# Two half exchanges through DRAM joined into one pair, in a gated graph network

## The chip, the cores and the metric

One core of a Trainium2 chip. The metric is the device time of one execution in microseconds. The kernel before took 1796.03 us in the median of three runs (1793.29 to 1797.85).

## What is computed

Sixteen graphs ("batches") of 1024 nodes with 128 features each, and a symmetric 0/1 adjacency matrix per graph. First a layer norm with relu and four layers of a gated graph network (GRU); then layer norm, relu, and four graph convolutions with batch norm over all graphs. Both results are added to the running `x`. The change lies in the GRU part:

```python
def _gru_cell(m, h, w_ih, w_hh, b_ih, b_hh):
    ...
    r = jax.nn.sigmoid(xr + hr)
    z = jax.nn.sigmoid(xz + hz)
    n = jnp.tanh(xn + r * hn)
    return (1.0 - z) * n + z * h
...
h = x
for i in range(L):                                     # L = 4
    hw = jnp.einsum('bnc,cd->bnd', h, weight[i])
    m = jnp.einsum('bjn,bjd->bnd', adj, hw)
    h = _gru_cell(m, h, w_ih[i], w_hh[i], b_ih[i], b_hh[i])
```

## The kernel before, in words

The path that runs is `exact_path`; a second, general path stands behind a flag and isn't entered. The kernel keeps `h` transposed (128 features on partitions, 1024 nodes along the row), in two halves of 512 nodes. The weight is folded into the input gates (`w_mT`), so that a layer first aggregates `h` over the adjacency and then runs the gates.

**Two streams.** `sa` takes the even batches and `sb` the odd ones. One `half_step(one, two)` runs the gates of stream `two` for its layer (`gate_step` for each half, L972 on TensorE: 24 matmuls) and then the aggregation of stream `one` for its next layer (`agg_step`, L525: 32 matmuls). Half steps alternate the roles. A batch takes four layers, so eight half steps make a round in which both streams change their batch, and there are seven such changes (fourteen batch ends, all but the last two batches).

**What the aggregation needs.** Its weights are `ghw`: `h` with the nodes on partitions, split into a high part (rounded, cast on ScalarE, L905) and a low part (the difference, on VectorE, L906). TensorE takes for each block of 128 nodes two matmuls of the high part and two of the low part, so it needs the low part of the first half two matmuls after the high one.

**The turn through DRAM.** For layers 1 to 3 the turn from features to nodes is made in two moves: VectorE transposes 32x32 blocks (`t_h`, L711), and SP dumps the result into a DRAM buffer (`exchange_out`, L591: one issue of 256 KB per half) and fetches it back with the blocks in another order (`exchange_in`, L598: four issues of 64 KB per half, each for 32 partitions). The buffers are called `cross_h`, the fetched tiles `n_h`. `half_away` makes the dumps after each half of the gates, `halves_back` issues the eight fetches at the start of the stream's next half step, and `split_back` makes `ghw` from them.

**The change of batches.** When a stream has done its fourth layer, `finish` does the same exchange for two more things: the coming batch's normalized `x` (`take`: `y_in` to `t_in` to `cross_in` to `h_in`), which the next gates read as `h`; and the last `h` of the batch that ends (`t_out` to `cross_out` and back into its own tile `h`), which VectorE adds to `x` in the tail (`tail_sums`, L732). `blocks_out` makes the two dumps of each. The fetches are put on an agenda with `at(clock[0] + 1, ...)`: those of `h_in` come first in the next half step (`due("ins")`), those of `h` after the first half of its gates and after the first dump of `half_away` (`due("outs")`).

**What sets the order.** In the steady part, the orders of TensorE, GpSimd and SP are those in which the program is written (`manual_schedule(engines=PE, Pool, SP)`). ScalarE's and VectorE's are chosen by a scheduler from its own cost estimates, so a change in the DMA issues can move instructions on these two. All SP issues stand in one queue: besides the exchanges, the row loads of the coming batch into `stage` (L573, eight per batch of 512 KB each, four buffers, so that the second four wait for the casts of the first), and DMA transposes of adjacency rows (L610). GpSimd casts each loaded row (L578, `row<-stage`) and each row to be transposed (L609, `half<-row`). ScalarE's `glance` (L587, `junk<-stage`) and VectorE's `look` (L604) test the loaded rows.

**DMA semaphores.** The issues of SP take eight completion semaphores in turn, so an issue also waits until the eighth issue before it has landed.

Of the kernel before, what the change touches and what calls it, by code (L numbers as in the profile page):

```python
# [8 lines left out]
F32 = mybir.dt.float32  # L9
# [7 lines left out]
P = 128  # L17
HALF = 512
# [323 lines left out]
def exact_path(  # L342
# [21 lines left out]
    nc = tc.nc  # L364
# [3 lines left out]
    NH = N // HALF  # L368
# [26 lines left out]
    def half_tile(name):  # L395
        return keep.tile([P, N], BF16, tag="half", name=name, bufs=8)
# [67 lines left out]
    turned = {}  # L464
# [69 lines left out]
    with ExitStack() as st:  # L534
        work = st.enter_context(tc.tile_pool(name="work", bufs=2))
        rawd = st.enter_context(tc.tile_pool(name="rawd", bufs=2, space=bass.MemoryType.DRAM))
# [49 lines left out]
                k = b * NB + j  # L586
                nc.scalar.activation(junk, lows, AF.Copy, accum_out=low[:, k : k + 1])  # L587

        def exchange_out(t, name):
            d = rawd.tile([P, HALF], F32, tag="cross", name=f"cross_{name}", bufs=8)  # L590
            nc.sync.dma_start(d, t)  # L591
            return d

        def exchange_in(d, t):

            src = d.rearrange("(t r) (s x) -> s r t x", t=4, s=4)
            for s in range(4):
                nc.sync.dma_start(t[s * 32 : (s + 1) * 32, :].rearrange("r (t x) -> r t x", t=4), src[s])  # L598

        def look(b, row, j, part=0):  # L600

            lows = row.bitcast(U16).rearrange("p (n t) -> p n t", t=2)[:, :, 0]
            k = (b + part * B) * NB + j
            nc.vector.tensor_reduce(low[:, k : k + 1], lows, axis=AX.X, op=ALU.max)  # L604
# [95 lines left out]
        def by_nodes(cols):  # L700
            return cols.rearrange("c (q k i) -> c k q i", q=4, i=32)

        def four_ways(cols):
            return cols.rearrange("p (k a c) -> p k a c", a=4, c=32)

        def blocks_out(src, name):

            return [half_out(cross_tile(f"t_{name}_{hf}"), src, hf, name)[0] for hf in range(NH)]

        def half_out(t, src, hf, name):  # L710
            turned = nc.vector.transpose(by_nodes(t), four_ways(src[:, hf * HALF : (hf + 1) * HALF]))  # L711
            return exchange_out(t, f"{name}_{hf}"), turned

        def cross_tile(name):
            return half_tile(name).bitcast(F32)
# [32 lines left out]
        def last_tail(b, xt, hT):  # L748
            nt = tail_sums(b, xt, hT)
            y = y_mid(b) if b + 1 < B else xt.rearrange("p k c -> p (k c)")  # L750
            store_xmid(b, xt)

            def rest():
                norm_apply(xt, y, nt)
                store_ymid(b, y)

            return rest
# [10 lines left out]
        class Stream:  # L768
# [105 lines left out]
            def take(self):  # L874
                self.xt, self.y = self.next_x, self.next_y
                self.across = True
                self.hT = work.tile([P, N], F32, tag="h", name=f"h_in{self.b}", bufs=7)
                return blocks_out(self.y, f"in{self.b}")
# [5 lines left out]
            def half_away(self, hf):  # L884

                if self.turned_away(self.i + 1 - hf):
                    nm = f"{self.b}_{self.i + 1 - hf}"
                    out, self.last_dve = half_out(cross_tile(f"t_h{nm}_{hf}"), self.new, hf, f"h{nm}")
                    self.outs.append(out)

            def halves_back(self):
                nm = f"{self.b}_{self.i}"
                self.backs = [cross_tile(f"n_h{nm}_{hf}") for hf in range(NH)]
                for d, t in zip(self.outs, self.backs):
                    exchange_in(d, t)
                self.hw = hw_tiles(self.b, f"ghw{nm}")
# [107 lines left out]
            def finish(self):  # L1004

                if self.i < L:
                    return
                args = self.b, self.xt, self.hT
                self.b, self.i = self.b + 2, 0
                if self.b >= B:  # L1010
                    self.rest = last_tail(*args)
                    return
                ins = self.take()
                h_in = self.hT
                outs = blocks_out(args[-1], f"out{args[0]}")
                parts = [args[-1][:, hf * HALF : (hf + 1) * HALF] for hf in range(NH)]

                def arrive(ds, ts):
                    for d, t in zip(ds, ts):
                        exchange_in(d, t)  # L1020

                at(clock[0] + 1, "ins", lambda: arrive(ins, [h_in[:, :HALF], h_in[:, HALF:]]))
                at(clock[0] + 1, "outs", lambda: arrive(outs, parts))
                self.plan(clock[0], (*args, parts))

        clock = [3]

        def at(n, place, go):
            agenda.setdefault((n, place), []).append(go)
# [268 lines left out]
    def first_weights(b, pm, stats):  # L1298

        mt = work.tile([P, N], F32, tag="h", name=f"cm{b}", bufs=3)  # L1300
        pc = [acc(t, f"pw{b}_{t}") for t in ("g_hn", "g_xn")]
        for hf in range(NH):
            cols = slice(hf * HALF, (hf + 1) * HALF)
            nc.scalar.copy(mt[:, cols], pm[hf])
            nc.tensor.matmul(pc[hf], w_c[:, 0, :], mt[:, cols], start=True, stop=True)
        return conv_done(b, 0, pc, stats)
# [70 lines left out]
    for b in range(B):  # L1377
# [4 lines left out]
        if waiting:  # L1382
            last = first_weights(*waiting, stats)
# [52 lines left out]
    for b in range(B):  # L1436
# [3 lines left out]
        for n0, n in pieces(b):  # L1440
# [5 lines left out]
            tag = turns[count % len(turns)]  # L1446
# [10 lines left out]
@with_exitstack  # L1457
def kernel(ctx: ExitStack, tc: tile.TileContext, *args):
    nc = tc.nc
    flagp = ctx.enter_context(tc.tile_pool(name="flagp", bufs=1))  # L1460
    flag_i = flagp.tile([1, 1], I32, tag="flag", name="flag_i")
    exact_path(tc, flag_i, *args)
    inexact = nc.values_load(flag_i, min_val=0, max_val=1 << 24)  # L1463
    with tc.If(inexact > 0):
        general_path(tc, *args)
# [41 lines left out]
```

## Time and profile before

| | before |
|---|---|
| median of 3 runs | 1796.03 us |
| span of the profiled execution | 1795.0 us |
| GRU part (to about 1130 us): TensorE busy | 1109.9 us |
| fetches of `h_in` from `cross_in` | 112 issues, 64 KB each, 2.2 us to landing (median) |
| fetches of `h` from `cross_out` | 112 issues, 64 KB each, 2.0 us |
| dumps `cross_in`, `cross_out` | 28 each, 256 KB, 6.8 and 7.0 us |
| fetches of `n_h` | 360 issues, 64 KB each, 2.0 us |

The profiled execution's own time is known by its span, from the first to the last instruction; the median of the runs lies 1.0 us above it. In the profile, a line such as `L525 PE MATMUL pm<-row,ghw` names the source line, the engine, the operation and the tiles, output first. In a timeline, the first two columns are start and duration in microseconds, `xN` says how many like instructions were merged, and the bracket is how long the engine had been idle and what ended the wait. PE is TensorE, PEld its weight load, ACT ScalarE, DVE VectorE, POOL GpSimd; `SPq` are issues of SP's queue. In a table by stretches, each engine has its busy time and its instructions.

### The profile page before, as it was taken

How to read it: one execution, taken by the hardware profiler on the slowest of the kernel's cores; microseconds unless marked ns; L12 is line 12 of the kernel's file. 1: busy time of each engine (PE TensorE's matmuls, PEld its weight loads, DVE VectorE, ACT ScalarE, POOL GpSimd, SP SyncE). 2: the span in 40 equal slices, each digit the busy share in tenths (PEclk: the TensorE clock that was granted, in tenths of full speed). 3: DMA queues.
4: the chain of work that ended last, by engine and by line, in shares of the span. 5: the costliest groups of instructions: out<-in, count | busy, mean ns of one | idle time of the engine just before them, and what ended most of it. 6: DMA issues, size and time to landing. Idle time of an engine off the chain costs nothing. (4 is left out here: it accounts for less than half of the span.)

```text
span 1795.0 us, 22286 instructions
## 1 busy us (share of the span) xinstructions
PE 1763.4 (98%) x6742; PEld 1194.0 (67%) x6742; DVE 1258.8 (70%) x2308; ACT 1107.2 (62%) x1717; POOL 389.4 (22%) x417
## 2 busy tenths in 40 slices
PE   9999999999999999999999999999999999999997
PEld 6555565556565556556556555677778888888886
DVE  7567867867776776777786776676666666666665
ACT  5346456556556555755655655477777767768765
POOL 4213322332332331422342333110100000000011
PEclk9999999999999999999999999999999999999999
DMA  7448676776676766766767667778866566767667
GB/s 253 112 125 268 171 223 237 200 207 225 205 211 211 236 191 193 263 197 168 263 185 209 241 194 209 268 277 299 284 223 244 209 244 215 246 223 240 241 220 263
DMA packets 363968, 399.11 MB, mean 222 GB/s; under 512 B 159820, under 2 KB 240496, under 8 KB 363840
## 3 DMA queue, kind: packets, MB, share of 16 engines
q1 hardware_dynamic: 343088, 322.54, 57.1%
q0 software_dynamic: 20224, 74.80, 11.5%
q8 instruction: 55, 0.90, 0.2%
q14 instruction: 73, 0.60, 0.1%
q10 hardware_dynamic: 528, 0.26, 0.0%
HBM read 266.95 MB, written 96.99 MB: 203 GB/s over the span
## 5 line engine op out<-in xcount | busy, mean ns | idle before, releaser
L525 PE MATMUL pm<-row,ghw 128*128 128x512 f32 x2048 | 505.6, 403 | 11.8 <-ACT ghw L905 11.1
L525 PEld LDWEIGHTS pm<-row,ghw 128*128 128x128 f32 x2048 | 384.3, 189 | 124.5 <-issue 26.5
L525 PE MATMUL pc_m<-wide,chw 128*128 128x512 f32 x1024 | 246.1, 396 | 0.0
L609 POOL CAST half<-row 128x1024 bf16<-128x1024 f32 x128 | 148.8, 1171 | 327.2 <-DMA adjT<-half 312.5
L525 PEld LDWEIGHTS pc_m<-wide,chw 128*128 128x128 f32 x1024 | 190.5, 188 | 42.3 <-issue 4.3
L991 ACT ACTIVATE z<-g_z,brz 128x512 f32<-128x512 f32 x128 | 87.5, 684 | 171.3 <-PE g_z L972 171.2
L525 PE MATMUL pc_g_r<-wide,chw 128*128 128x512 f32 x464 | 187.0, 403 | 0.3 <-ACT chw L502 0.3
L578 POOL CAST row<-stage 128x1024 fp32r<-128x1024 f32 x112 | 131.5, 1181 | 243.6 <-DMA stage<-in_adj_dram 221.1
L525 PE MATMUL pc_g_z<-wide,chw 128*128 128x512 f32 x464 | 181.0, 390 | 0.0
L985 DVE SCALAR_TENSOR_TENSOR r<-g_hn,vecs,r 128x512 f32<-128x512 f32 x128 | 95.0, 742 | 118.3 <-ACT r L984 76.6
L1237 DVE CAST wide<-block 128x1024 fp32r<-128x1024 bf16 x160 | 109.8, 692 | 73.2 <-PE pc_m L525 46.2
L1237 DVE CAST wide<-packed 128x1024 fp32r<-128x1024 bf16 x160 | 110.2, 691 | 72.1 <-PE pc_g_z L525 53.9
L944 ACT COPY m<-pm 128x512 f32<-128x512 f32 x128 | 68.5, 586 | 147.9 <-PE pm L525 147.9
L990 ACT ACTIVATE r<-r,vecs 128x512 f32<-128x512 f32 x128 | 91.8, 717 | 104.0 <-DVE r L986 104.0
L997 DVE TENSOR_TENSOR h<-h,r 128x512 f32<-128x512 f32 x96 | 81.8, 852 | 101.6 <-ACT r L990 101.6
L1235 ACT CAST wide<-packed 128x1024 fp32r<-128x1024 bf16 x96 | 100.6, 1048 | 59.1 <-PE pc_m L525 28.3
L972 PE MATMUL g_r<-m,w_mT 128*128 128x512 f32 x256 | 131.5, 595 | 2.8 <-ACT m L944 2.3
L1235 ACT CAST wide<-block 128x1024 fp32r<-128x1024 bf16 x96 | 100.6, 1049 | 52.3 <-PE pc_g_z L525 27.7
L972 PE MATMUL g_xn<-m,w_mT 128*128 128x512 f32 x256 | 130.7, 592 | 0.0
L972 PE MATMUL g_z<-m,w_mT 128*128 128x512 f32 x256 | 130.7, 592 | 0.0
L998 DVE TENSOR_TENSOR h<-h,z 128x512 f32<-128x512 f32 x128 | 118.7, 931 | 4.8 <-ACT z L991 1.9
L1285 DVE BATCH_NORM_STATS2 stats<-feat 128x6 f32<-128x512 f32 x128 | 84.1, 686 | 47.0 <-ACT feat L1284 45.9
(187 smaller groups left out, 2804.3 us busy)
## 6 DMA issues: line engine op xcount, KB each, us to landing
block<-adjT_d SPq DMA_DIRECT2D x256, 256.0 KB, 4.7
packed<-adjT_d SPq DMA_DIRECT2D x256, 256.0 KB, 5.5
stage<-in_adj_dram SPq DMA_DIRECT2D x120, 512.0 KB, 4.8
adjT_d<-adjT POOLq DMA_DIRECT2D x16, 2048.0 KB, 8.3
cross_h<-t_h SPq DMA_DIRECT2D x90, 256.0 KB, 3.2
n_h<-cross_h SPq DMA_DIRECT2D x360, 64.0 KB, 2.0
xmid_d<-x POOLq DMA_DIRECT2D x16, 512.0 KB, 5.4
y<-ymid_d POOLq DMA_DIRECT2D x16, 512.0 KB, 5.9
```

Of the source, the lines that this page charges most:

```text
L525: nc.tensor.matmul(pm[hf], hw[s][:, j * P : (j + 1) * P], rows[j][:, hf * HALF : (hf + 1) * HALF], start=(j == 0 and s == 0), stop=(j == N ...
L578: nc.gpsimd.tensor_copy(t, stage[j % 4])
L609: nc.gpsimd.tensor_copy(t, row.bitcast(F32))
L972: nc.tensor.matmul(po, wT[:, i, g * C : (g + 1) * C], rhs, start=start, stop=stop)
L985: nc.vector.scalar_tensor_tensor(r, phn, b_hn(i), r, ALU.add, ALU.mult)
L990: nc.scalar.activation(r, r, AF.Tanh, bias=b_in(i))
L991: self.last_act = nc.scalar.activation(z, pz, AF.Sigmoid, bias=brz[:, 3 * i + 1 : 3 * i + 2])
L997: nc.vector.tensor_sub(ho, hin, r)
L998: nc.vector.tensor_mul(ho, ho, z)
L1235: nc.scalar.copy(r, t)
L1237: nc.vector.tensor_copy(r, t)
L1285: nc.vector.bn_stats(stats[:, b * NH + hf, :], dst)
```

## The change

A DRAM buffer `pair` of two halves takes the place of two `cross` buffers at a batch's end. The dumps stay as they were, one for each half, into the halves of the pair. The fetch is made for both halves at once: four issues of 128 KB, each for 32 partitions and eight runs of 512 bytes per partition, where there were eight of 64 KB. It is done for `h_in` and for `h`, at the same places of the agenda. `n_h`, between the layers, keeps its eight fetches.

```diff
-        def exchange_out(t, name):
-            d = rawd.tile([P, HALF], F32, tag="cross", name=f"cross_{name}", bufs=8)
+        def exchange_out(t, name, d=None):
+            if d is None:
+                d = rawd.tile([P, HALF], F32, tag="cross", name=f"cross_{name}", bufs=8)
             nc.sync.dma_start(d, t)
             return d
...
+        def pair_in(d, t):
+
+            src = d.rearrange("h (t r) (s x) -> s r (h t) x", t=4, s=4)
+            for s in range(4):
+                nc.sync.dma_start(t[s * 32 : (s + 1) * 32, :].rearrange("r (a x) -> r a x", a=8), src[s])
...
         def blocks_out(src, name):
 
-            return [half_out(cross_tile(f"t_{name}_{hf}"), src, hf, name)[0] for hf in range(NH)]
+            d = rawd.tile([NH, P, HALF], F32, tag="pair", name=f"pair_{name}", bufs=4)
+            for hf in range(NH):
+                half_out(cross_tile(f"t_{name}_{hf}"), src, hf, name, d[hf])
+            return d
...
-                def arrive(ds, ts):
-                    for d, t in zip(ds, ts):
-                        exchange_in(d, t)
-
-                at(clock[0] + 1, "ins", lambda: arrive(ins, [h_in[:, :HALF], h_in[:, HALF:]]))
-                at(clock[0] + 1, "outs", lambda: arrive(outs, parts))
+                last = args[-1]
+                at(clock[0] + 1, "ins", lambda: pair_in(ins, h_in))
+                at(clock[0] + 1, "outs", lambda: pair_in(outs, last))
```

More of the change, by code (lines that the diff above doesn't have):

```diff
@@ L706, in blocks_out, with half_out @@
         def blocks_out(src, name):
-            return [half_out(cross_tile(f"t_{name}_{hf}"), src, hf, name)[0] for hf in range(NH)]
-        def half_out(t, src, hf, name):
+            d = rawd.tile([NH, P, HALF], F32, tag="pair", name=f"pair_{name}", bufs=4)
+            for hf in range(NH):
+                half_out(cross_tile(f"t_{name}_{hf}"), src, hf, name, d[hf])
+            return d
+        def half_out(t, src, hf, name, d=None):
             turned = nc.vector.transpose(by_nodes(t), four_ways(src[:, hf * HALF : (hf + 1) * HALF]))
-            return exchange_out(t, f"{name}_{hf}"), turned
+            return exchange_out(t, f"{name}_{hf}", d), turned
         def cross_tile(name):
```

## The prediction

> **What bounds the kernel now.** I read the page first, then TensorE's own waits, then busy time by step, then the timeline of one step, engine by engine.
>
> ```profile
> PE 1763.4 (98%) x6742; PEld 1194.0 (67%) x6742; DVE 1258.8 (70%) x2308; ACT 1107.2 (62%) x1717; POOL 389.4 (22%) x417
> ```
>
> PE is the bound. So a change to DMA issues can only pay where PE waits, and PE's waits (columns: total us, times, longest) are few:
>
> ```profile
> PE pm L525 <- ACT ghw L905: 11.1, 7, 2.8
> ...
> PE g_r L972 <- ACT m L944: 2.3, 3, 1.0
> ```
>
> Seven waits, one per change of batches. The timeline places them at 202.93, 348.79, 491.64, 634.46, 777.51, 921.36 and 1066.73 us, idle 1.28 (+0.33 on VectorE), 1.93, 1.28, 1.28, 1.28, 1.28 and 2.80: 11.46 us. I call a round's half steps A (first gates after `sa` has finished), B (gates of the new `sa` batch) and C (gates of the new `sb` batch, then the aggregation of `sa`'s layer 1, where PE waits). B and C of the third round, stretch by stretch:
>
> ```profile
> 462.31:479.89 17.58, 17.58 (x58) 10.57 (x56) 13.48 (x17) 10.37 (x19) 7.62 (x6) 1.00 0.73 228
> 479.89:499.30 19.41, 18.13 (x57) 10.41 (x56) 16.66 (x41) 7.77 (x13) 6.17 (x7) 1.00 0.68 190
> ```
>
> Same matmuls, 19.41 against 17.58: a stall costs 1.83 us where it shows 1.28 of idle, because the last gate matmul's drain (0.57) otherwise lies under its successor. So the seven cost 11.46 + 7 x 0.57 = 15.4 us. That is all there is to gain. What each engine does in C of that round:
>
> ```profile
> 479.48 0.34 SPq L591 DMA_DIRECT2D cross_h<-t_h  x1
> 479.92 3.73 SPq L598 DMA_DIRECT2D h<-cross_out  x8
> 483.74 0.38 SPq L591 DMA_DIRECT2D cross_h<-t_h  x1
> 484.25 2.63 SPq L610 DMA_TRANSPOSE adjT<-half  x2
> 486.93 4.07 SPq L598 DMA_DIRECT2D n_h<-cross_h  x8
> ```
> ```profile
> 490.39 0.69 ACT L991 ACTIVATE z<-g_z,brz 128x512 f32<-128x512 f32 x1 [2.75 <-PE g_z L972]
> 490.98 0.61 ACT L905 CAST ghw<-n_h 128x512 fp32r<-128x512 f32 x1
> 493.01 0.62 ACT L905 CAST ghw<-n_h 128x512 fp32r<-128x512 f32 x1 [1.42 <-DMA n_h<-cross_h]
> ```
> ```profile
> 478.76 1.29 DVE L711 STREAM_TRANSPOSE t_h<-h 128x512 f32<-128x512 f32 x2
> ...
> 487.35 1.41 DVE L998 TENSOR_TENSOR h<-h,z 128x512 f32<-128x512 f32 x1
> 488.68 0.74 DVE L985 SCALAR_TENSOR_TENSOR r<-g_hn,vecs,r 128x512 f32<-128x512 f32 x1
> ...
> 491.62 0.69 DVE L906 TENSOR_TENSOR ghw<-n_h,ghw 128x512 fp32r<-128x512 f32 x1 [0.20 <-ACT ghw L905]
> ```
>
> SP sends the second dump of `h` (483.74) only after the eight fetches from `cross_out`, though its data stood ready at 480.05. Behind it stand two transposes and the eight `n_h` fetches that PE needs. ACT's first `ghw` cast stands behind the second `z`, which waits for PE's last gate: PE must therefore wait for `z` and the cast, even with the data there. That, not the data, made the 1.28 of four rounds.
>
> [...] 64 KB `n_h` fetches land after 2.0 us (median), 256 KB `cross_h` dumps after 3.2. [...] `h_in` fetches land after 2.2 us in the median, and after 8.0 behind 512 KB row loads. [...] `h*z` takes 1.41 us at 487.35, beside a POOL cast at 487.10, and 0.69 at 495.83 without one.
>
> **The change, part by part.**
> *Issues.* 14 batch ends lose 8 fetch issues each: 112 of about 0.47 us (3.73/8), 52 us of SP's time. SP isn't the bound, so this is worth nothing by itself; the cover is SP's idle time. The dumps (56) stay.
> *Bigger fetches.* A 128 KB fetch isn't in the trace. Bounds: 2.0 us (a 64 KB one) and 3.2 (a 256 KB dump). I take 2.3[...].
> *Later start.* A fetch now waits for both dumps, and every reader for all four fetches. For `h_in` in B: the first four issues stood at 474.14, on the landing of the first dump; the second dump is issued 0.67 us later (1.07 for two), so four fetches run 474.8 to 476.7 and land by 479.0. The gates that read them start at 479.89. Cost nothing, margin 0.9 us here; if the margin is overrun, PE waits for the excess. Queued behind on SP is only the `cross_h` dump, whose data came at 479.4. In A, `h_in` (eight issues from 451.85, 7.79 long, held back by row loads landing) loses four, and isn't later. `h` from `cross_out` is read by VectorE's tail sums a step later: nothing.
> *SP in C.* Four issues fewer before the second `cross_h` dump: 4 x 0.47 = 1.9 us. Dump, transposes and `n_h` follow 1.9 earlier: the first half of `n_h`, now landed about 490.6 (fourth issue ends 489.1, plus the tail of its 2.0), at 488.7, the second near 491.1 for 493.0.
> *SP in A.* Eight issues fewer stand before the second four row loads (`stage`, at 464.58): they can go once the row before is cast (POOL ended at 460.7) and the fetches are out, near 460, 4 to 5 us earlier. So POOL's row casts and the two `half` casts after them (474.75 to 477.69) are over near 472, not 477.7.
> *ACT and DVE orders.* They are set by the scheduler, and the built kernel shows them moved in each round: in B two glances (`junk`) ahead of the second `tanh`, not one; in C `tanh` ahead of the first `z`, the first `ghw` cast ahead of the second `z`, on VectorE `h+r` ahead of the second half's `r` and the transpose ahead of its next `r`. The counts are unchanged. One added glance (1.05 + 0.19 us, less the 0.7 of idle there) delays `tanh` in B by about 0.5 us. In D, one `ghw` subtraction goes two places back; PE takes it 3.9 us after its start: nothing.
>
> **Step C worked out again.** With PE never waiting, the aggregation starts at 489.79 (last gate matmul's start 489.76) and needs ACT's cast by then and VectorE's low part 0.47 later (two matmuls), at 490.26. Cast: data at 488.7, ACT free since 487.65, done by 489.4: in time. VectorE: in B, after 472.5 and free of POOL, `h-r`, two `h*z` (2.96 merged), two `h+r` (2.12) shrink to 0.7 each, so `t_h` ends near 478 where it ended at 480.05; tail sums and statistics (4.2 us) end by 482.5. From there each operation follows PE: g_hn of the second half ends at 487.78, then `r` 0.74, transpose 0.69, `r` 0.68, low part 0.69, with the small overlaps that the trace shows: 490.5. PE waits about 0.3 us, where the stall cost 1.85.
> Rounds 1 to 6: costs 1.61+0.57, 1.93+0.57 and 4 x 1.85 = 12.1; left 6 x 0.3 = 1.8; gain 10.3. Round 7 differs: VectorE is held to 1050.06 by the `worst` reduction waiting for the last glance, which the new order doesn't hasten. Its low part then comes near 1066.3, so PE's start moves from 1066.73 to about 1065.9: gain 0.8. Sum 11.1. The profiled span is 1795.0, so 1783.9; the median of the runs, 1796.0, lies 1.0 above that span, which gives **1785 us**. With every stall gone it would be 1796.0 - 15.4 = 1780.6.
>
> **Rivals.** (a) VectorE stays late: POOL's casts, started by the earlier transposes, fall on C's `h-r` and `h*z`, as at 487.35 now. Then the low part comes at 491.1 to 491.7, PE's start at 490.7 to 491.3 instead of 491.64: 0.3 to 0.9 in a round, with about 1 in the first, second and last. 4 x 0.6 + 3 = 5.4 or less: about 1791. For it: the doubled times exist already. Against: the row loads have 4 us to move.
> (b) The change does nothing that PE sees: `n_h` still lands near 490.6, because transposes wait for POOL or the link is taken. PE then starts as now: 1796. For it: POOL waits 312.5 us on the transposes. Against: their casts are done at 477.69, before their turn.
> (c) Slower, by whole-tile arrival: `h_in` no longer comes in halves, and PE's first gate needs all of it. It decides when the second dump lands after 475.6 in B of round three (479.89 - 1.9 - 2.4; now about 474.7). Dumps already take 6.8 us in the median, behind row loads. If they come 2 us later, PE waits 1.1 us in seven rounds, nothing of the stall need remain to pay it: with the gain of (b), 1796 + 7.7 = 1804. Against: the row loads ahead of those dumps move earlier, not later.
>
> **How the numbers follow.** Forecast 0.55 (1780.6 to 1788), (a) 0.20 (1788 to 1793.5), (b) 0.12 (1793.5 to 1798), (c) 0.13 (1798 to 1806). 0.3% is 5.4 us, about what this measurement can tell from no change. Faster by more: 0.55 and half of (a), 0.65. Within: the other half and (b), 0.22. Slower: 0.13. The range takes the forecast, (a) and part of (b): 1780.5 to 1795.
>
> **What would show it.** Right: PE's waits on `ghw` at most 3 us in total where they were 11.1, left on VectorE's `ghw` and in the last round; C lasts about 17.9 us; the second `cross_h` dump follows its fetches by 1.9 us less; `stage` loads in A start 4 us earlier. Wrong: a new wait of `g_r` on `h_in`; `h*z` still 1.41 in C; `n_h` landing unmoved; or a stall of like size in step A or D.

## The result and the profile after

The kernel after takes 1787.29 us in the median of five runs (1784.79 to 1787.94). The ratio to the kernel before is 0.9945, with a 95% interval from 0.9933 to 0.9956: 0.55% faster. (The kernel before has five runs here as well; its median is still 1796.03 us.) The profiled execution has a span of 1786.2 us, where before had 1795.0; the median lies 1.1 above it.

The busy times of the page, then TensorE's waits for the operands of the GRU part (total us, times, longest):

```profile
PE 1761.1 (99%) x6742; PEld 1193.5 (67%) x6742; DVE 1254.0 (70%) x2308; ACT 1107.5 (62%) x1717; POOL 387.7 (22%) x417
```
```profile
PE pm L525 <- DVE ghw L916: 4.1, 5, 2.1
PE g_r L982 <- ACT m L954: 3.2, 4, 1.0
...
PE pm L525 <- ACT ghw L915: 0.2, 1, 0.2
```

The instruction counts are the same. The seven waits on ScalarE's `ghw` (11.1 us) are down to one of 0.2. What is left stands on VectorE's low part (4.1), half of it one wait of 2.1 in round seven. The waits of the gates on `m`, nearly all in step A, are 0.9 us more.

Step C of rounds three, six and seven, by stretches (from and to, length, then busy time and instructions of PE, PEld, DVE, ACT and POOL, then granted clock, busy share of the DMA engines and GB/s):

```profile
474.44:492.44 18.00, 17.89 (x57) 10.49 (x56) 14.75 (x33) 7.76 (x13) 6.74 (x7) 1.00 0.65 173
901.31:919.89 18.58, 17.87 (x58) 10.49 (x57) 16.06 (x33) 7.76 (x13) 7.21 (x7) 1.00 0.77 167
1044.33:1066.19 21.86, 19.53 (x58) 11.41 (x57) 20.67 (x54) 7.77 (x13) 7.06 (x7) 0.92 0.70 192
```

A step without a stall takes 17.57. The third round's C costs 18.00 where it cost 19.41; the sixth keeps 1.01 too much, the seventh 4.29. In the seventh the granted clock is 0.92: that line holds a second cause beside the stall, taken up below.

The same step C of round three, engine by engine. First SP, then ScalarE, then VectorE (start, duration):

```profile
471.30 0.34 SPq L592 DMA_DIRECT2D cross_h<-t_h  x1
471.74 1.89 SPq L605 DMA_DIRECT2D h<-pair_out  x4
473.73 0.40 SPq L592 DMA_DIRECT2D cross_h<-t_h  x1
474.24 2.69 SPq L617 DMA_TRANSPOSE adjT<-half  x2
476.97 3.90 SPq L599 DMA_DIRECT2D n_h<-cross_h  x8
```
```profile
482.10 0.61 ACT L915 CAST ghw<-n_h 128x512 fp32r<-128x512 f32 x1
484.94 0.69 ACT L1001 ACTIVATE z<-g_z,brz 128x512 f32<-128x512 f32 x1 [2.24 <-PE g_z L982]
```
```profile
479.68 1.11 DVE L1005 TENSOR_TENSOR h<-h_in,r 128x512 f32<-128x512 f32 x1 [0.84 <-ACT r L1000]
480.89 0.69 DVE L1008 TENSOR_TENSOR h<-h,z 128x512 f32<-128x512 f32 x1
481.62 0.69 DVE L1009 TENSOR_TENSOR h<-h,r 128x512 f32<-128x512 f32 x1
482.44 0.75 DVE L995 SCALAR_TENSOR_TENSOR r<-g_hn,vecs,r 128x512 f32<-128x512 f32 x1
483.11 0.70 DVE L721 STREAM_TRANSPOSE t_h<-h 128x512 f32<-128x512 f32 x1
483.73 0.65 DVE L996 TENSOR_TENSOR r<-g_xn,r 128x512 f32<-128x512 f32 x1
484.31 1.12 DVE L916 TENSOR_TENSOR ghw<-n_h,ghw 128x512 fp32r<-128x512 f32 x1
```

The four fetches take 1.89 us of SP where eight took 3.73, and the `n_h` fetches begin 2.5 us after the step's first gate (474.44), not 7.0. ScalarE's first cast runs at 482.10, before the second `z`, 2.2 us ahead of TensorE's need at 484.34. VectorE then decides: its low part starts at 484.31, behind two operations of the second half (both write `r`) and the first half's transpose. TensorE asks for it two matmuls after 484.34, and waits. The three operations L1005, L1008 and L1009, which close the gates of a half, are called `h-r`, `h*z` and `h+r` below.

### The profile page after: what moved, and what is told of

The parts are those of the page before. It is cut to its first block, busy times and chain, and to the rows that moved or that the text cites. A ratio compares the mean times of both kernels' runs of the same rounds, so it can differ in the third digit from the quotient of the medians.

```text
span 1786.2 us, 22134 instructions
## 1 busy us (share of the span) xinstructions
PE 1761.1 (99%) x6742; PEld 1193.5 (67%) x6742; DVE 1254.0 (70%) x2308; ACT 1107.5 (62%) x1717; POOL 387.7 (22%) x417
## 3 DMA queue, kind: packets, MB, share of 16 engines
q0 software_dynamic: 20224, 74.80, 11.4%
## 5 line engine op out<-in xcount | busy, mean ns | idle before, releaser
L616 POOL CAST half<-row 128x1024 bf16<-128x1024 f32 x128 | 145.0, 1143 | 336.2 <-DMA adjT<-half 321.5
L994 ACT ACTIVATE r<-g_r,brz 128x512 f32<-128x512 f32 x128 | 87.8, 686 | 37.4 <-PE g_r L982 37.1
```

Of the source, the lines that this page charges most:

```text
L616: nc.gpsimd.tensor_copy(t, row.bitcast(F32))
L994: self.first_act = nc.scalar.activation(r, pr, AF.Sigmoid, bias=brz[:, 3 * i : 3 * i + 1])
```

## The experiments

"Excess" is the length of a step C over 17.57, summed over the seven rounds: 17.0 us before, 7.95 after. The kernel before, run beside the experiments, took 1798.15 us (first four kernels) and 1798.05 (last two).

**Only the last `h` in a pair.** `h_in` keeps its two buffers and eight fetches (`blocks_out` with `False` makes the two dumps of before).

```diff
-                at(clock[0] + 1, "ins", lambda: pair_in(ins, h_in))
+                at(clock[0] + 1, "ins", lambda: arrive(ins, [h_in[:, :HALF], h_in[:, HALF:]]))
...
-            return blocks_out(self.y, f"in{self.b}")
+            return blocks_out(self.y, f"in{self.b}", False)
```

> Only the last h goes through a pair (four fetches); h_in keeps its eight of 64 KB. Built, ScalarE and VectorE stand in the order of the kernel before, and SP has four issues fewer ahead of the second cross_h dump in step C. So this is the DMA saving of step C without the new order. My theory (the order releases PE, the DMA saving only lets it): the 1.28 us stalls of rounds 3 to 6 stay, since the first ghw cast still stands behind the second z; only what was DMA beyond that goes in rounds 1, 2 and 7, together about 3 us: 1793 us, PE's wait on ghw about 9 us. Rival (fewer issues alone did it): 1788 us, PE's wait on ghw about 4.

Measured: 1798.3 us, ratio 1.0005 (0.9995 to 1.0014). Excess 17.39. No gain. TensorE's waits, and ScalarE in step C of round three (it starts at 479.31):

```profile
PE pm L525 <- ACT ghw L917: 9.0, 7, 1.3
...
PE pm L525 <- DVE ghw L918: 2.8, 5, 1.1
```
```profile
486.38 0.69 ACT L996 ACTIVATE r<-g_r,brz 128x512 f32<-128x512 f32 x1 [0.42 <-PE g_r L984]
489.82 0.69 ACT L1003 ACTIVATE z<-g_z,brz 128x512 f32<-128x512 f32 x1 [2.75 <-PE g_z L984]
490.40 1.13 ACT L917 CAST ghw<-n_h 128x512 fp32r<-128x512 f32 x2
```

In this kernel ScalarE's and VectorE's orders are those of before. The first half of `n_h` landed 7.2 to 8.2 us after the start of step C in rounds one to six, where it had been 9.1 to 11.6. The cast could have run from 487.1 on; it stands behind `z`, and ScalarE idles 2.75 us for that `z`. So fetches that land 1.7 to 3.7 us earlier are worth nothing in the old order. The 1793 us of the theory did not come. In rounds two and seven the high part comes earlier (waits of 1.28 us, not 1.93 and 2.80), but TensorE then waits for the low part, and it does so in rounds three, five and six as well (2.8 us in five waits). All waits on `ghw` together are 11.8 us, where they were 11.4.

**Only `h_in` in a pair.** The mirror image: the last `h` keeps its eight fetches.

```diff
-                outs = blocks_out(args[-1], f"out{args[0]}")
+                outs = blocks_out(args[-1], f"out{args[0]}", False)
...
-                at(clock[0] + 1, "outs", lambda: pair_in(outs, last))
+                at(clock[0] + 1, "outs", lambda: arrive(outs, parts))
```

> Only h_in goes through a pair; the last h keeps its eight fetches. Built, ScalarE and VectorE stand exactly in the order of the changed kernel, while SP still has eight fetches ahead of the second cross_h dump in step C (in A four fewer stand before the row loads). My theory: most of the gain is here, because the order lets PE start before the second z; n_h comes later than in the changed kernel, so about 2 us of the 9 are missing: 1789 us. Rival (the DMA saving in step C did it): 1795 us, stalls as before.

Measured: 1788.61 us, ratio 0.9949 (0.9936 to 0.9961), excess 8.06. Its orders on ScalarE and VectorE are those of the kernel after.

```profile
PE g_r L984 <- ACT m L956: 2.3, 3, 1.0
PE pm L525 <- ACT ghw L917: 2.2, 2, 1.8
```

This half of the change brings nearly all of the gain (0.9949 against 0.9945, and the intervals overlap). The four issues saved ahead of the second `cross_h` dump in step C are worth next to nothing: `n_h` lands later than in the kernel after (7.9 to 10.0 us from the start of C in rounds one to six, against 6.0 to 8.0), and only the 2.2 us of waits on ScalarE show it, most of them in round seven. The theory's 1789 us came; its reason, 2 us lost by the later data, is not shown, for so small a difference is not clear of the noise.

**The old DMAs in the new order.** The kernel before, with its operations in step C held by hints in the order of the kernel after. For the second half, `hold` names the first half's `h+r`, its transpose and the first `ghw` cast; for the first half, `z` stands behind `tanh`.

```diff
-                nc.vector.scalar_tensor_tensor(r, phn, b_hn(i), r, ALU.add, ALU.mult)
-                self.mid_dve = nc.vector.tensor_add(r, pxn, r)
+                with behind(*(() if hold == "z" else hold[:1])):
+                    nc.vector.scalar_tensor_tensor(r, phn, b_hn(i), r, ALU.add, ALU.mult)
+                with behind(*(() if hold == "z" else hold[1:2])):
+                    self.mid_dve = nc.vector.tensor_add(r, pxn, r)
...
-                    nc.scalar.activation(r, r, AF.Tanh, bias=b_in(i))
-                self.last_act = nc.scalar.activation(z, pz, AF.Sigmoid, bias=brz[:, 3 * i + 1 : 3 * i + 2])
+                    tanh = nc.scalar.activation(r, r, AF.Tanh, bias=b_in(i))
+                with behind(*([tanh] if hold == "z" else hold[2:3])):
+                    self.last_act = nc.scalar.activation(z, pz, AF.Sigmoid, bias=brz[:, 3 * i + 1 : 3 * i + 2])
```

> The exchanges of the kernel before, untouched (SP's queue is the same line by line), and in step C the order of the changed kernel on ScalarE (tanh ahead of the first z, first ghw cast ahead of the second z) and on VectorE (h+r ahead of the second half's r, transpose ahead of its next r), forced by order hints alone. My theory (both are needed): n_h lands as late as before, 0.3 us before the old start of the cast, so each stall shrinks by some 0.3 us, and by nothing in rounds 2 and 7: 1794 us. Rival (the order alone is the gain): 1788 us.

Measured: 1794.49 us, ratio 0.998 (0.9972 to 0.9987), excess 14.98.

```profile
PE pm L525 <- ACT ghw L905: 7.7, 7, 2.4
...
PE pm L525 <- DVE ghw L906: 1.5, 3, 0.6
```
```profile
485.08 0.68 ACT L985 ACTIVATE r<-g_r,brz 128x512 f32<-128x512 f32 x1
489.26 0.62 ACT L905 CAST ghw<-n_h 128x512 fp32r<-128x512 f32 x1 [3.51 <-DMA n_h<-cross_h]
489.79 0.68 ACT L995 ACTIVATE z<-g_z,brz 128x512 f32<-128x512 f32 x1
```

Here the cast stands ahead of the second `z`, and now it waits 3.51 us for its data (step C from 477.87). The 1794 us of the theory came, but not round by round: rounds five and six gained 1.0 and 1.1 us, where the theory had 0.3, and round three became 0.6 longer. With the first experiment this makes a table of two by two, in ratios to the kernel before: early data in the old order 1.0005, late data in the new order 0.998, both 0.9945. The two together are worth more than their sum. The table is not quite clean: the first experiment has the pair of the last `h` alone, the third has the new order in step C alone, and no run has both pairs in the old order. That the order is needed rests on the 2.75 us in which ScalarE stood before `z` with the data of the cast already landed.

**The low part ahead of the second half's `r`.** The kernel after, with one hint in step C: for the second half, `hold` is the low part of the first half of `ghw`.

```diff
-                nc.vector.scalar_tensor_tensor(r, phn, b_hn(i), r, ALU.add, ALU.mult)
+                with behind(*hold):
+                    nc.vector.scalar_tensor_tensor(r, phn, b_hn(i), r, ALU.add, ALU.mult)
```

> The changed kernel, and in step C VectorE makes the low part of the first half before the second half's r (an order hint). What is left of the stall in the changed kernel waits for that low part (4.1 us, and each stall some 0.5 more than it shows). My theory: that rest goes in rounds 1 to 6, about 3.7 us, and about half of the 4.3 of the last round: 1782 us, PE's wait on VectorE's ghw under 1.5 us. Rival (PE is held by something else there, for instance the landing of n_h, and VectorE is only named because it is last): 1787 us, the wait then named on ScalarE's cast or a DMA.

Measured: 1782.6 us, ratio 0.991 (0.9896 to 0.9924). The excess is 0 in rounds one to six and 1.86 in the seventh. Of the 2.4 us that the seventh gained, 1.4 are a low clock that did not come this time (see the last section), which the theory had not meant.

```profile
PE g_r L983 <- ACT m L955: 3.5, 5, 1.0
...
PE pm L525 <- DVE ghw L916: 1.2, 1, 1.2
```
```profile
482.78 0.71 DVE L721 STREAM_TRANSPOSE t_h<-h 128x512 f32<-128x512 f32 x1
483.41 0.65 DVE L916 TENSOR_TENSOR ghw<-n_h,ghw 128x512 fp32r<-128x512 f32 x1
483.98 0.74 DVE L997 SCALAR_TENSOR_TENSOR r<-g_hn,vecs,r 128x512 f32<-128x512 f32 x1
```

The low part is ready at 484.06, and the aggregation of this round starts at 484.56 and runs 32 matmuls without a break. With the low part, the transpose went ahead of that `r` too. So the rest of up to 1.0 us per round goes with VectorE's order alone; it was not the landing of `n_h`.

**`worst` moved away.** Why does round seven gain nothing? VectorE's line in step B of that round in the kernel after, and, beside it in C, its operations and GpSimd's casts:

```profile
1040.23 0.30 DVE L1223 TENSOR_REDUCE worst<-low 128x1 f32<-128x144 f32 x1 [3.93 <-ACT junk L587]
...
1051.87 1.34 DVE L1005 TENSOR_TENSOR h<-h_in,r 128x512 f32<-128x512 f32 x1 [0.84 <-ACT r L1000]
1053.32 1.34 DVE L1008 TENSOR_TENSOR h<-h,z 128x512 f32<-128x512 f32 x1
```
```profile
1051.63 2.48 POOL L616 CAST half<-row 128x1024 bf16<-128x1024 f32 x2 [14.92 <-DMA adjT<-half]
```

The edit puts the reduction behind the GRU part:

```diff
-    nc.vector.tensor_reduce(worst, low, axis=AX.X, op=ALU.max)
+    with tc.issue_after(sb.last_dve.ins):
+        nc.vector.tensor_reduce(worst, low, axis=AX.X, op=ALU.max)
```

> The kernel after with one edit: the reduction `worst`, on which VectorE waits 3.93 us for the last glance in step B of round seven, is put behind the whole GRU part. Theory: that wait is what spoils round seven. In the kernel after it holds VectorE until 1040.23, while the operands of `h-r` and `h*z` stand ready near 1037.4; so `t_h`, its dump and the two DMA transposes are some 3.5 us late, and GpSimd's `half` casts fall at 1051.63 upon `h-r` and `h*z` of step C (1.34 us each in place of 0.69). Without it round seven goes like the rounds before: its step C, now 4.29 us over the 17.57 of a step without a stall, is left with about 0.7, and the time is 1787.3 - 3.6 = 1783.7 us, 0.993 of before, with PE's waits on VectorE's `ghw` near 2.0 us in place of 4.1. Rival: the order of step C in that round, the second half's `r` ahead of the low part, makes the wait whatever VectorE did before; then step C keeps over 3 us, and the time stays near 1787, 0.994.

Measured: 1785.1 us, ratio 0.9928 (0.9914 to 0.9942). Step C of rounds three and seven, and VectorE in round seven's B and C:

```profile
475.20:493.54 18.34, 17.87 (x58) 10.49 (x57) 15.57 (x33) 7.77 (x13) 6.78 (x7) 1.00 0.65 171
1045.89:1064.24 18.35, 17.88 (x57) 10.48 (x56) 15.73 (x35) 7.76 (x13) 6.70 (x7) 1.00 0.66 171
```
```profile
1039.75 1.29 DVE L1008 TENSOR_TENSOR h<-h,z 128x512 f32<-128x512 f32 x2
...
1051.13 1.26 DVE L1005 TENSOR_TENSOR h<-h_in,r 128x512 f32<-128x512 f32 x1 [0.84 <-ACT r L1000]
1052.49 0.69 DVE L1008 TENSOR_TENSOR h<-h,z 128x512 f32<-128x512 f32 x1
```

Round seven now costs what the third does: an excess of 0.78 for 4.29, as the theory had it. Of these 3.5 us, 1.65 are TensorE's busy time (17.88 for 19.53), most of it the low clock that did not come. The rival said that step C would keep over 3 us: it is refuted by the step. The time alone does not tell this kernel from the kernel after, since the intervals overlap (0.9933 to 0.9956 there). The waits on VectorE's `ghw` did not fall to the 2.0 us expected: they are 3.8, since the other rounds have excesses of 0.6 to 1.4 here instead of 0 to 1.0. In sum that is 1.4 us more, as much as the time lies above 1783.7; single runs of this kernel are up to 5 us apart, though.

**Both edits.**

> Both edits: the low part of the first half ahead of the second half's `r` in step C, and `worst` behind the GRU part. Theory: the two repair different things, the low part in rounds one to six and the wait for the last glance in round seven. The one step C that the first edit left with a stall, 1.86 us in round seven, goes, and the time is 1782.6 - 1.9 = 1780.7 us, 0.990 of before; no wait of PE on `ghw` is left, only those of step A on `m` and what `h_in` may cost. This is as well what the forecast's best case gave, 1780.6, with every stall of step C gone. Rival: with VectorE free earlier in step B of round seven, something else is last there, the landing of `n_h` behind the row loads or the tail of the last batch, and the time stays at 1782.6.

Measured: 1778.67 us, ratio 0.9896 (0.988 to 0.9911). Round seven's step C:

```profile
1039.57:1057.15 17.58, 17.58 (x58) 10.56 (x57) 13.87 (x33) 7.78 (x13) 6.10 (x7) 1.00 0.70 185
```

No wait of TensorE on `ghw` is left in any step C, all seven excesses are 0, and the fastest kernel of the study is 1.04% below before. It lies 2 us under the expected 1780.7; in the profiles, step A, which the edits were not meant for, is 0.9 us shorter in sum than in the fourth experiment. Two waits of step A on `m` (1.0 us each) remain.

## Why the prediction was right, and where its sum was off

It gave 1785 and named a chain that the runs confirm but for one link; 2.3 us of the expected 11.1 are missing. Its own signs came out mixed. The waits on `ghw` are 4.3 us in total, where at most 3 would have been right. Step C takes 17.6 to 18.6 us in rounds one to six, for about 17.9. The second `cross_h` dump follows its fetches by 1.8 us less, and the row loads of step A are early. Two of the signs of being wrong came too, both small: one wait of `g_r` on `h_in` (0.2 us), and `h*z` in step C at 1.30 to 1.42 us in rounds two, four, six and seven. Point by point:

*What there was to gain.* The 15.4 us of stalls are right to the tenth, but they aren't all of the excess. Step C of round one before:

```profile
191.18:212.53 21.35, 19.74 (x58) 11.55 (x56) 19.24 (x47) 7.76 (x13) 6.65 (x7) 0.92 0.71 195
```

TensorE is busy 19.74 us there and 18.13 in the other rounds, at a granted clock of 0.92: 1.6 us that the working didn't see. 17.0 - 1.6 = 15.4. The kernel after has the same once, in round seven: 19.53 - 18.13 = 1.4. So the stalls fell from 15.4 to 7.95 - 1.4 = 6.55, a gain of 8.85; the clock gave 0.2.

*The orders on ScalarE and VectorE.* Right, and needed: without them early data gained nothing (first experiment), and with them late data gained little (third). The prediction read them from the built kernel. It did not say which half of the change moves them: it is the pair of `h_in`.

*SP in A.* Right and too small: in round three the second four row loads come 13.3 us after the start of step A, not 20.3, so 7 us earlier where 4 to 5 were expected. Before, fetch issues stood 24.9 us on SP, in 19 waits of at most 2.2, until a row load had landed. Of SP's 1547 issues with a landing in that trace, none starts before the eighth ahead of it has landed, and 261 start before the seventh has. What follows from the earlier loads, VectorE free of GpSimd's casts in step B, holds: `h*z` and `h+r` take 1.29 and 1.28 us for both halves, not 2.96 and 2.12. Here is `h*z` before and after:

```profile
473.82 2.96 DVE L998 TENSOR_TENSOR h<-h,z 128x512 f32<-128x512 f32 x2
```
```profile
468.16 1.29 DVE L1008 TENSOR_TENSOR h<-h,z 128x512 f32<-128x512 f32 x2
```

*SP in C.* The four issues saved are there (1.9 us), and `n_h` lands 1.0 to 4.8 us earlier in rounds one to six, not 1.9, because `t_h` is ready earlier as well: in round three it ends 2.6 us before the first gate of step C, where it had ended 0.2 us after it. But as a step of the sum the four issues were needless: without them (second experiment) the time is the same within the intervals.

*The bigger fetch.* Taken at 2.3 us. In step B, with no row loads ahead, the four `h_in` fetches land after 2.2 to 2.7. Those of step A, the other half, stand behind row loads and land after 6.8 to 8.9; the median over all is 4.7. They cost TensorE one wait of 0.2 us, at the start of step B of round five. Rival (c), whole-tile arrival, came to no more than that.

*The rest of 0.3 us per round.* This term was too small: 0.71, 0.68, 0.43, 0.83, 0.01 and 1.01 us in rounds one to six, 3.67 for 1.8. The working let VectorE run step C free of GpSimd. It doesn't. In round six, first VectorE, then GpSimd; in round three, the cast that meets the low part of 484.31:

```profile
906.54 1.49 DVE L1005 TENSOR_TENSOR h<-h_in,r 128x512 f32<-128x512 f32 x1 [0.84 <-ACT r L1000]
908.13 1.34 DVE L1008 TENSOR_TENSOR h<-h,z 128x512 f32<-128x512 f32 x1
```
```profile
906.45 2.48 POOL L616 CAST half<-row 128x1024 bf16<-128x1024 f32 x2 [14.16 <-DMA adjT<-half]
```
```profile
483.84 1.04 POOL L616 CAST half<-row 128x1024 bf16<-128x1024 f32 x1 [3.60 <-DMA adjT<-half]
```

In rounds two, four and six two of the operations `h-r`, `h*z` and `h+r` are stretched beside `half` casts, and the low part starts 0.7 to 0.9 us later than in round five. In rounds one and three the low part itself takes 1.39 and 1.12 us beside a cast. In round five it starts 0.1 us ahead of the cast and takes 0.67: the excess is 0.01. That is rival (a)'s mechanism, on more operations than it named, in every one of these rounds that kept an excess. Beside the two casts of round six `h-r` and `h*z` take 1.49 and 1.34 us, where the `h*z` of round three at 480.89, with no cast beside it, takes 0.69. Whether it reaches TensorE is a matter of VectorE's order: in the fourth experiment `h-r` or `h*z` is stretched in every round (1.30 to 1.54 us), and with the low part earlier the excess of rounds one to six is 0.

*Round seven.* The gain was put at 0.8 us, and the step got 0.92 longer. Without the clock's 1.4 the stall is 2.89 for 3.37: a gain of 0.5. The reason given, `worst` holding VectorE, is the one that the fifth experiment confirms. What the step missed is that the low clock may fall into another round.

*The sum.* Step C gave 17.0 - 7.95 = 9.05. Step A lost 1.2 (excess 5.4 before, 6.6 after), a cost that the prediction put at nothing. Over all kernels here it goes with one half of the change: it is 5.0 to 5.4 us in the three that keep eight fetches for the last `h`, and 5.6 to 7.0 in the five that fetch it as a pair. With one profile of each, and single steps between 0 and 1.9 us, this is a link and not a shown cause; why it should be so stays open. About 0.5 us each came at the start and after the last round, and no term of the working names them: that much of the hit is luck. 9.05 - 1.2 + 1.0 = 8.85, and the spans differ by 8.8.

## What to carry to other kernels

When a saved transfer frees an in-order engine, ask which instruction stands in front of the one that reads its data: in the old order, data that landed 1.7 to 3.7 us earlier was worth nothing, and in the new order with old data most of the stall stayed. Where a scheduler sets the orders, read the built kernel's, since the edit that moves them need not be the one with the larger saving. And when one operand's stall has gone, look at once for the next operand of the same matmuls: here, one hint on the low part added more than half as much again to the gain (0.991 for 0.9945).

## What was not expected of the hardware

Behind one stall of the kernel after, the clock granted to TensorE fell as well, to 0.65 over 4 us. In round seven, around the wait of 2.08 us that ends at 1057.88:

```profile
1050.00:1055.00 5.00, 4.79 (x12) 1.81 (x10) 3.91 (x5) 2.50 (x5) 2.48 (x2) 1.00 0.73 173
1055.00:1058.00 3.00, 0.88 (x3) 0.42 (x3) 3.00 (x6) 1.92 (x3) 0.35 (x1) 0.90 0.79 187
1058.00:1062.00 4.00, 4.00 (x12) 3.21 (x13) 3.93 (x4) 1.58 (x2) 3.19 (x4) 0.65 0.83 252
1062.00:1066.19 4.19, 4.19 (x21) 3.42 (x20) 4.16 (x15) 0.04 (x1) 1.04 (x1) 1.00 0.54 155
```

In stretches of 2 us the lowest is 0.50. Apart from the last microseconds of each execution, where the clock is 0.50 as well, the same happens exactly once in the profiles of before (round one, after waits of 1.28 and 0.33 us), of the first three experiments (rounds five, seven and seven; it is part of their excesses), and nowhere in the last three, whose longest wait at a change of batches is 1.20 us. Each costs 1.4 to 1.8 us of busy time. The length of the wait alone doesn't decide: one of 2.80 us before, in round seven, went without it, as did most of those of 1.28. What decides which stall is hit stays open.
